# Starting the last stage of a three-stage graph kernel beside the second convolution's last closings, with the early edge terms split over two generators

## The chip, the cores and the metric

The kernel runs on 1 core of one Trainium2 chip. The metric is the device time of one execution in microseconds (us), lower being better. TensorE is called PE in the profile, VectorE DVE, ScalarE ACT, GpSimd POOL, and SP is the queue engine that issues most DMAs.

## The reference, cut to what matters

There are N = 12,500 nodes with 64 features, E = 200,000 edges sorted by destination, and 64 features on every edge.

```python
h = relu(layernorm(x))
g = relu(sage(h, W1l, W1r, b1))          # first convolution
x = x + sage(g, W2l, W2r, b2)            # second convolution
h = relu(layernorm(x))
# last stage, one message for every edge
m = relu(concat(h[src], h[dst], edge_attr) @ W1 + b1) @ W2 + b2
x = x + segment_mean(m, src)

def sage(x, Wl, Wr, b):
    mean = segment_sum(x[src], dst) / max(count(dst), 1)
    return mean @ Wl.T + b + x @ Wr.T
```

## The kernel before, in words

**Tiles and cells.** Nodes are put into 49 blocks of 256. The edges are sorted on the chip into 49 x 49 = 2401 cells, one for each pair (destination block, source block), with 128 slots. Gathers and segment sums are matmuls with one-hot matrices: `turned` (line 741) is made on VectorE from a row of node numbers that is spread over all partitions (`srow`, `drow`, line 731), and `hot` (line 750) from a column of them.

**Three stages.** The two convolutions are one loop over parts of 16 cells (lines 947 to 967): for each group of 4 cells, line 896 gathers into `got`, ScalarE copies it to `rows` (line 900), and three groups later line 775 adds it into a PSUM sum `acc`. `acc` has two buffers. Each time a row of 49 cells is full, a closing `conv` (lines 812 to 843) runs for that block of 256 nodes: a copy of the sums, a mean, a transposition (834), a matmul with the weights (839), and then `after_conv1` or `after_conv2`. The latter loads x (855), adds it (858), does a layer norm and makes the two tables of the last stage, `ta` and `tb` (864 to 884). The last stage (line 1144 on) goes in groups of 8 cells: matmuls into `got` (1077, 1078), `y` = gathered values plus edge terms (1081, 1083), ReLU (1086), two subtractions on GpSimd (1089), and sums three groups later by line 775. It goes through the 40 early source blocks in its first 1960 cells, and through the 9 late ones in the other 441.

**What sets the order.** Nothing is scheduled by a compiler: each engine executes its instructions in the order in which the Python code issues them. Steps are written as generators. `Line.tick` moves every open group or closing on by one `yield`, so that the work of several groups is mixed on each engine. `ahead` (line 911) loads the `srow`/`drow` of the first two parts, makes the first part's `turned`, and later loads two parts ahead.

**Edge terms.** `edge_terms` (lines 355 to 426) computes edge_attr @ W1 beside the main work. It loads edges of 4 blocks (3 blocks for the late ones) at a time by four (three) DMAs (369), transposes 4 (3) tiles (399), copies them (405), multiplies them (414), copies the result to `terms_o` (422) and then scatters it into DRAM tables by indirect DMAs on GpSimd's queue (382), each with an index column `turn_i` copied on VectorE (381). A unit of 4 tiles takes six steps and eight scatters. The class `Beside` takes a step whenever the cells passed, times a weight, add up to its pace: 4.45 per step with weights 1.1 and 0.9 per cell in the two convolutions, and 6.2 per step with weight 1 in the last stage. `rest()` takes all steps that are left at once. The early edge terms are 60 loads in one generator, which starts at cell 152 of the first convolution and goes on in the second. Its index table `pos` lies in the same pool, `terms`, on the right side of SBUF. Under this pacing it takes its last step at cell 2300 of the second convolution. The late generator takes its last step at cell 1904 of the last stage. When a generator ends, the scatters that are left are issued in one go (line 425).

**Between the stages.** After the second convolution's loop, line 968 takes all closings to their end, lines 969 and 970 reload what is left of `tb`, and only then do the pools `layers` (left side) and `terms` close and the pools of the last stage open. A pool that is opened where others were closed makes its first users wait for the last users of the old ones.

Of the kernel before, what the change touches and what calls it, by code (L numbers as in the profile page):

```python
# [9 lines left out]
FT = mybir.dt.float32  # L10
BF = mybir.dt.bfloat16
I32 = mybir.dt.int32
# [3 lines left out]
P = 128  # L16
# [98 lines left out]
def fast_path(  # L115
# [20 lines left out]
    N, D = x.shape  # L136
# [4 lines left out]
    NB = -(-N // BLK)  # L141
# [3 lines left out]
    CH = 7  # L145
# [16 lines left out]
    BJ = 5  # L162
    EARLY = J * BJ * HALVES
    LATE = NB - EARLY
    assert LATE > 0
# [188 lines left out]

    def edge_terms(work, psum, groups, ITEMS, U):


        loads = []
        for blocks in groups:
            step = ITEMS // len(blocks)  # L360
            loads += [(blocks, t0, min(step, TG - t0)) for t0 in range(0, TG, step)]

        def load(blocks, t0, m):
# [25 lines left out]
        before = iter(())  # L389
        ahead = load(*loads[0])  # L390
        for at, (blocks, t0, m) in enumerate(loads):
            e = ahead
# [32 lines left out]
        for _ in before:  # L425
            pass

# [70 lines left out]
    terms_work = terms_in.enter_context(tc.tile_pool(name="terms", bufs=2, side="right"))  # L498
    pos = terms_work.tile([P, EARLY, T], I32, name="pos", bufs=1)

    def pos_of(B):
        return pos[:, B] if B < EARLY else pos_late[:, B - EARLY]

# [219 lines left out]

    groups = [[*range(q, q + J)] for q in range(0, EARLY, J)]
    beside = Beside(edge_terms(terms_work, psum_x, groups, 12, 4), 4.45)


# [79 lines left out]
    work = layers.enter_context(tc.tile_pool(name="layers", bufs=2))  # L807
    next_rows = rows_with_one(work)
    line = Line()
    second = [None]  # L810

    def conv(layer, table, w, b, finish, B, acc):

        yield
        v = work.tile([P, 2, W3], FT, name="sums")
        nc.scalar.copy(v, acc[:, :, :W3])
        yield
        m = work.tile([P, 2, 2, D], FT, name="both")
        t = table[:, B]
# [13 lines left out]
        for h in range(2):  # L833
            nc.tensor.transpose(acc[:, h, :P], m[:, h].rearrange("p a d -> p (a d)"), ident)
        ct = work.tile([P, 2, P], FT, name="both_t")
        nc.scalar.copy(ct, acc[:, :, :P])
        yield
        for h in range(2):
            nc.tensor.matmul(acc[:, h, P:P + D], ct[:, h], w, start=True, stop=True)  # L839
        o = work.tile([P, 2, D], FT, name="conv")  # L840
        nc.vector.tensor_add(o, acc[:, :, P:P + D], rows(b, 2))
# [8 lines left out]
    def after_conv2(B, o):  # L850
# [31 lines left out]
        yield  # L882
        if not last:
            nc.sync.dma_start(of_block(b_mem, B), b)
            stored.add(B)
# [24 lines left out]

    def ahead(todo, load, turn):


        loaded = [load(p) for p in todo[:2]]
        made = {0: turn(todo[0], loaded[0])}
        for _ in made[0][1]:
# [11 lines left out]

    gathered, stored, present = [0], set(), set()

    def again():
        new = [B for B in range(gathered[0]) if B in stored and B not in present]
        if new and (len(new) >= CH or not line.all):
            B0 = new[0]
            B1 = next(B for B in range(B0, NB + 1) if B not in new or B == B0 + CH)
            nc.sync.dma_start(tb[:, B0:B1],
                              b_mem[B0 * BLK:B1 * BLK].rearrange("(b p h) d -> p b h d", p=P, h=2))
            present.update(range(B0, B1))
            return True

# [6 lines left out]
    for (layer, c0, c1, part), t, coming in ahead(  # L947
            todo, lambda p: sources(*p[:3]),
            lambda p, r: turned(work, "turned", r, p[2] - p[1])):
        for a, z in part:  # L950
# [6 lines left out]
            if layer or a >= 150:  # L957
                beside.passed((z - a) * (1.1, 0.9)[layer])
            if layer:
                gathered[0] = max(z - (CELLS - NB), 0)  # L960
                again()
        if layer == 0 and c1 == CELLS:
            for _ in chain(sorter, clearing):
                pass
            nc.vector.tensor_copy(which, bad)
            sorting.close()
            second[0] = layers.enter_context(tc.tile_pool(name="second", bufs=2))
    line.finish()
    while again():
        pass  # L970
    assert present == set(range(NB))
    beside.rest()
    layers.close()
    terms_in.close()

# [5 lines left out]
    late_in = ExitStack()  # L981
    late_work = late_in.enter_context(tc.tile_pool(name="late", bufs=2, side="right"))
    beside = Beside(edge_terms(late_work, psum_x, [[*range(B, min(B + LJ, NB))] for B in range(EARLY, NB, LJ)], 12, 3), 6.2)

    def keep(K, acc):

        v = late_work.tile([P, 2, W3], FT, name="sums")
        nc.scalar.copy(v, acc[:, :, :W3])
# [73 lines left out]
    def messages(last, e, p, ts, td, c0, a, z):  # L1062
# [3 lines left out]
        for c in range(n):  # L1066
            K, f = divmod(a + c, F)
            B = order[last][f]
            at = slice((a - c0 + c) * S, (a - c0 + c + 1) * S)
            for i, (lt, rt) in enumerate(((ts[:, 0, at], ta[:, K, 0]), (ts[:, 1, at], ta[:, K, 1]),  # L1070
# [35 lines left out]

    line = Line()
    summed = []

    under_way = [None]  # L1110
# [33 lines left out]
    for (last, c0, c1, part), (e, ts, td), coming in ahead(  # L1144
            [(last, *p) for last in range(2) for p in parts(G3, NB * len(order[last]))],
            lambda p: tuple(wait_rows(work, n, r[p[0]], p[1], p[2])
                            for n, r in (("srow", srow_k), ("drow", drow_k))), turned_both):
        if last and c0 == 2 * PART:
# [4 lines left out]
        for a, z in part:  # L1153
            around(lambda: line.tick_behind(messages(
                last, e, gather.tile([P, G3, 2 * D], FT, name="got"), ts, td, c0, a, z)))
            for _ in range(2):
                next(coming, None)
            if not last:
                beside.passed(z - a)
# [268 lines left out]
```

## Time and profile before

| | us |
|---|---|
| median of 3 runs | 3727.71 (3725.05 to 3731.02) |
| the profiled execution's own time | 3723.96 |
| its span in the trace | 3722.1 |
| first convolution, first to last gather | 93 to 1338 |
| second convolution, first to last gather | 1340 to 2305 |
| last stage, first matmul to the end | 2328 to 3722 |

| engine | busy us | share of the span |
|---|---|---|
| PE matmul | 3505.5 | 94% |
| PE weight load | 3423.2 | 92% |
| DVE | 3322.8 | 89% |
| POOL | 2732.6 | 73% |
| ACT | 2568.7 | 69% |

Shares are averages over three stages, so what a change in one place is worth has to be read from that place: from a table of busy time in chosen stretches, and from the list of instructions in order of time with the idle time before each of them and what ended it. In that list, "[4.11 <-DMA edges]" means that the engine had been idle for 4.11 us and that the landing of `edges` ended it. "PEclk" in the table of stretches is the share of TensorE's full clock that was granted.

### The profile page before, as it was taken

Reading aid. Unit: us, or ns where it says so; the run is one execution under the profiler, and the core shown is the slowest. Engines: PE = TensorE matmul, PEld = TensorE weight load, DVE = VectorE, ACT = ScalarE, POOL = GpSimd, SP = SyncE. Lnnn points to the kernel's source line nnn. Section 1 sums busy time; section 2 is a strip of 40 time slices with the busy share of each in tenths; the row PEclk is TensorE's granted clock in tenths of the full one; section 3 lists DMA queues with packets and bytes.
Section 4 is the critical chain, followed back from the end, with each engine's and each line's share of the span. In section 5 each row is a group of like instructions: output and inputs, shape, how many; then the busy total and the mean of one; then the engine's idle time right before and its main releaser. Section 6 shows DMA issues by size and latency. Waiting matters only on the chain.

```text
span 3722.1 us, 130679 instructions
## 1 busy us (share of the span) xinstructions
PE 3505.5 (94%) x51318; PEld 3423.2 (92%) x51318; DVE 3322.8 (89%) x7346; ACT 2568.7 (69%) x5875; POOL 2732.6 (73%) x2306
## 2 busy tenths in 40 slices
PE   1799999999999999999999998999999999998987
PEld 0799999999999999999999998899999999998887
DVE  7899999999999978888888887899999999998998
ACT  3466666666666667777777776688888888876665
POOL 4057787777778777777777774688888888996454
PEclk9999999999999999999999999999999999999999
DMA  6654555555454344444444444666666666666664
GB/s 209 247 169 148 159 153 157 156 157 156 137 166 151 116 129 141 136 136 144 136 131 140 139 132 131 227 215 203 217 214 212 203 216 210 208 196 193 196 213 138
DMA packets 413697, 635.90 MB, mean 171 GB/s; under 512 B 94131, under 2 KB 296247, under 8 KB 413070
## 3 DMA queue, kind: packets, MB, share of 16 engines
q1 hardware_dynamic: 353106, 572.87, 48.7%
q0 software_dynamic: 53312, 51.36, 4.6%
q8 instruction: 402, 6.59, 0.7%
q10 hardware_dynamic: 6652, 3.24, 0.4%
q14 instruction: 225, 1.84, 0.2%
HBM read 474.72 MB, written 155.83 MB: 169 GB/s over the span
## 4 chain that ended last, share of the span: by engine, by line
PE 75%; DVE 15%; DMA 4%; issue 3%; ACT 2%; POOL 1%; SPq 1%; DVEq 0%; POOLq 0%; ACTq 0%
PE acc L775 26%; PE got L896 17%; PE got L1077 11%; PE got L1078 6%; PE pE L414 4%; DVE hot L750 3%; DVE turned L741 2%; PE pE L399 2%; DVE hot_r L635 2%; PE pX L645 2%; DVE turned_d L741 1%; DMA terms_in<-terms 1%; PE acc L839 1%; PE got L1074 1%; PE pX L617 1%
## 5 line engine op out<-in xcount | busy, mean ns | idle before, releaser
L382 POOL DMA_INDIRECT terms<-terms_o,turn_i x1666 | 1937.7, 1163 | 663.3 <-issue 220.5
L900 ACT CAST rows<-got 128x384 bf16<-128x384 f32 x2402 | 1038.5, 487 | 592.3 <-PE got L896 577.7
L775 PEld LDWEIGHTS <-hot 128*128 128x128 bf16 x12006 | 1029.5, 98 | 19.0 <-issue 7.9
L775 PE MATMUL acc<-rows,hot 128*128 128x193 bf16 x9604 | 1006.0, 247 | 0.7 <-DVE hot L750 0.7
L1089 POOL TENSOR_TENSOR hidden<-hidden 128x512 f32<-128x512 f32 (+1 forms) x602 | 756.3, 1257 | 259.6 <-ACT hidden L1086 179.3
L896 PEld LDWEIGHTS <-turned 128*128 128x128 bf16 x9604 | 814.7, 98 | 67.4 <-issue 27.5
L750 DVE TENSOR_TENSOR hot<-dcol,local 128x1024 bf16<-128x1024 bf16 x1202 | 814.3, 682 | 4.1 <-PE acc L775 3.7
L741 DVE TENSOR_SCALAR turned<-srow,nid 128x2048 bf16<-128x2048 bf16 (+1 forms) x906 | 780.4, 875 | 21.1 <-issue 10.7
L1077 PE MATMUL got<-ta,turned 128*128 128x128 bf16 x3920 | 599.8, 220 | 7.3 <-DVE turned L741 7.3
L1077 PE MATMUL got<-tb,turned_d 128*128 128x128 bf16 x3920 | 600.7, 221 | 1.7 <-DVE turned_d L741 1.1
L1078 PE MATMUL got<-tb,turned_d 128*128 128x64 bf16 x3920 | 546.9, 193 | 0.0
L1078 PE MATMUL got<-ta,turned 128*128 128x64 bf16 x3920 | 546.5, 193 | 0.0
L896 PE MATMUL got<-ta,turned 128*128 128x192 bf16 x4802 | 499.7, 247 | 37.4 <-issue 24.8
L1097 ACT ACTIVATE hot_a<-every,scol 128x256 bf16<-128x256 bf16 x1200 | 507.0, 493 | 0.0
L896 PE MATMUL got<-tb,turned 128*128 128x192 bf16 x4802 | 494.1, 246 | 0.8 <-DVE turned L741 0.5
L1086 ACT ACTIVATE hidden<-y 128x512 f32<-128x512 f32 (+1 forms) x301 | 190.4, 632 | 293.5 <-DVE y L1083 169.5
L1077 PEld LDWEIGHTS <-turned 128*128 128x128 bf16 x3920 | 362.8, 98 | 8.2 <-issue 7.8
L1077 PEld LDWEIGHTS <-turned_d 128*128 128x128 bf16 x3920 | 360.2, 98 | 2.9 <-DVE turned_d L741 2.4
L1078 PEld LDWEIGHTS <-turned 128*128 128x128 bf16 x3920 | 359.5, 98 | 1.2
L1078 PEld LDWEIGHTS <-turned_d 128*128 128x128 bf16 x3920 | 359.9, 98 | 0.0
L741 DVE TENSOR_SCALAR turned_d<-drow,nid 128x2048 bf16<-128x2048 bf16 (+2 forms) x302 | 324.9, 1117 | 0.0
L1099 ACT ACTIVATE hot_a<-hot_a 128x1024 bf16<-128x1024 bf16 x300 | 317.2, 1057 | 9.5
(227 smaller groups left out, 5302.4 us busy)
## 6 DMA issues: line engine op xcount, KB each, us to landing
srow<-srow_b SPq DMA_DIRECT2D x300, 512.0 KB
srow<-srow_k SPq DMA_DIRECT2D x149, 512.0 KB
drow<-drow_k SPq DMA_DIRECT2D x149, 512.0 KB
terms_in<-terms SPq DMA_DIRECT2D x294, 160.0 KB
edges<-in_edge_attr_dram SPq DMA_DIRECT2D x200, 192.0 KB
terms<-tb SPq DMA_DIRECT2D x200, 160.0 KB
terms<-tb SPq DMA_DIRECT2D x48, 640.0 KB
terms<-terms_o,turn_i POOLq DMA_INDIRECT x1666
```

What stands on the lines that cost most here:

```text
L382: nc.gpsimd.indirect_dma_start(out=terms[j][:], out_offset=bass.IndirectOffsetOnAxis(ap=at, axis=0), in_=o[:, c, h], in_offset=None, bound ...
L741: nc.vector.tensor_scalar(o[:, h, :n * S], r[:, :n * S], nid[:, h:h + 1], None, op0=OP.is_equal)
L750: nc.vector.tensor_tensor(o[:, :n], cols.rearrange("p (g c) -> p g c", c=2).unsqueeze(2).to_broadcast([P, n, 2 * P, 2]), local.rearrange(" ...
L775: nc.tensor.matmul(self.acc[B][:, h, :W3], lt, r[:, c, 0:W3], start=k + h == 0, stop=k == row - 1 and h == 1, skip_group_check=True)
L896: nc.tensor.matmul(p[:, (i - c) * D3:(i - c + 1) * D3], t[:, h, (a - c0 + i) * S:(a - c0 + i + 1) * S], table[:, (a + i) % NB, h], start=h ...
L900: nc.scalar.copy(g[:, c:c + m, :D3], p[:, :m * D3].rearrange("p (c d) -> p c d", c=m))
L1077: nc.tensor.matmul(p[:, c], lt, rt[:, 0:2 * D], start=i == 0, stop=False, skip_group_check=True)
L1078: nc.tensor.matmul(p[:, c, 0:D], lt, rt[:, 2 * D:], start=False, stop=i == 3, skip_group_check=True)
L1086: nc.scalar.activation(w[:, :n, 0:D], y[:, :n], AF.Relu)
L1089: nc.gpsimd.tensor_sub(w[:, :n, (i + 1) * D:(i + 2) * D], w[:, :n, j], upper(w)[:, :n, j])
L1097: nc.scalar.activation(q[:, c - k], every, AF.Abs, scale=-1.0, bias=scol[:, scol_at[last] + a + c:scol_at[last] + a + c + 1])
L1099: nc.scalar.activation(q[:, :n - k], q[:, :n - k], AF.Relu, bias=1.0, scale=-2.0)
```

## The change

The early edge terms are made by two generators, of 33 and of 27 loads. The first is taken to its end when the first convolution ends (`beside.rest()`), and its pool closes. A new pool `second` is opened in that place, which holds the tiles of the second convolution's closings, and beside it a new pool `terms` for the second generator. The index table is split: blocks 0 to 19 in the old place, blocks 20 to 39 in `pos_second` in the pool `layers`. A generator begins with two empty steps behind its first load, and the last scatters of a generator are steps of their own. The weights go from 1.1 and 0.9 to 1.13 and 0.875.

At the end of the second convolution, closings are ticked only until the last sum is complete. Pools `terms` and `layers` close then, and the last stage begins: the first `srow` and `drow` loads, seven ticks of the closings, the first `turned`, and then four ticks behind each of the first groups of 8 cells, until no closing is left. Only then does the late generator start.

```diff
-    def edge_terms(work, psum, groups, ITEMS, U):
+    def edge_terms(work, psum, groups, ITEMS, U, only=slice(None)):
...
+        loads = loads[only]
...
         ahead = load(*loads[0])
+        yield
+        yield
...
         for _ in before:
-            pass
+            yield
...
-    pos = terms_work.tile([P, EARLY, T], I32, name="pos", bufs=1)
+    pos = terms_work.tile([P, J * BJ, T], I32, name="pos", bufs=1)
...
-    beside = Beside(edge_terms(terms_work, psum_x, groups, 12, 4), 4.45)
+    beside = Beside(edge_terms(terms_work, psum_x, groups, 12, 4, slice(FIRST)), 4.45)
...
+    pos_second.append(work.tile([P, J * BJ, T], I32, name="pos_second", bufs=1))
...
     def conv(layer, table, w, b, finish, B, acc):
 
+        work_ = second[0] if layer else work
...
-    def ahead(todo, load, turn):
+    def ahead(todo, load, turn, between=lambda: None):
 
         loaded = [load(p) for p in todo[:2]]
+        between()
...
-                beside.passed((z - a) * (1.1, 0.9)[layer])
+                beside.passed((z - a) * (1.13, 0.875)[layer])
...
             sorting.close()
-            second[0] = layers.enter_context(tc.tile_pool(name="second", bufs=2))
-    line.finish()
-    while again():
-        pass
-    assert present == set(range(NB))
+            beside.rest()
+            terms_in.close()
+            second[0] = seconds.enter_context(tc.tile_pool(name="second", bufs=2, side="right"))
+            terms_in = ExitStack()
+            terms_work = terms_in.enter_context(tc.tile_pool(name="terms", bufs=2, side="right"))
+            beside = Beside(edge_terms(terms_work, psum_x, groups, 12, 4, slice(FIRST, None)), 4.45)
     beside.rest()
+    gathered[0] = NB
+    while sums.acc:
+        line.tick()
+        again()
+    terms_in.close()
     layers.close()
-    terms_in.close()
+    ending, line = line, Line()
...
-            lambda p: tuple(wait_rows(...)), turned_both):
+            lambda p: tuple(wait_rows(...)), turned_both,
+            lambda: [ending.tick() for _ in range(7)]):
...
-            if not last:
+            if late_pool[0] is None:
+                for _ in range(4):
+                    ending.tick()
+                while again():
+                    pass
+                if not ending.all:
+                    assert present == set(range(NB))
+                    seconds.close()
+                    late_pool[0] = late_in.enter_context(tc.tile_pool(name="late", bufs=2, side="right"))
+                    beside = late(late_pool[0])
+            elif not last:
                 beside.passed(z - a)
```

More of the change, by code (lines that the diff above doesn't have):

```diff
@@ L163, in fast_path @@
     EARLY = J * BJ * HALVES
+    FIRST = 33
     LATE = NB - EARLY
@@ L498, in fast_path @@
     terms_work = terms_in.enter_context(tc.tile_pool(name="terms", bufs=2, side="right"))
-    pos = terms_work.tile([P, EARLY, T], I32, name="pos", bufs=1)
+    pos = terms_work.tile([P, J * BJ, T], I32, name="pos", bufs=1)
+    pos_second = []
     def pos_of(B):
-        return pos[:, B] if B < EARLY else pos_late[:, B - EARLY]
+        if B < J * BJ:
+            return pos[:, B]
+        return pos_second[0][:, B - J * BJ] if B < EARLY else pos_late[:, B - EARLY]
     sorting = ExitStack()
@@ L808, in fast_path @@
     next_rows = rows_with_one(work)
+    pos_second.append(work.tile([P, J * BJ, T], I32, name="pos_second", bufs=1))
     line = Line()
+    seconds = ExitStack()
     second = [None]
     def conv(layer, table, w, b, finish, B, acc):
+        work_ = second[0] if layer else work
         yield
-        v = work.tile([P, 2, W3], FT, name="sums")
+        v = work_.tile([P, 2, W3], FT, name="sums")
         nc.scalar.copy(v, acc[:, :, :W3])
         yield
-        m = work.tile([P, 2, 2, D], FT, name="both")
+        m = work_.tile([P, 2, 2, D], FT, name="both")
         t = table[:, B]
@@ L834, in conv @@
             nc.tensor.transpose(acc[:, h, :P], m[:, h].rearrange("p a d -> p (a d)"), ident)
-        ct = work.tile([P, 2, P], FT, name="both_t")
+        ct = work_.tile([P, 2, P], FT, name="both_t")
         nc.scalar.copy(ct, acc[:, :, :P])
@@ L839, in conv @@
             nc.tensor.matmul(acc[:, h, P:P + D], ct[:, h], w, start=True, stop=True)
-        o = work.tile([P, 2, D], FT, name="conv")
+        o = work_.tile([P, 2, D], FT, name="conv")
         nc.vector.tensor_add(o, acc[:, :, P:P + D], rows(b, 2))
@@ L882, in after_conv2 @@
         yield
-        if not last:
+        if last:
+            ready.add(B)
+        else:
             nc.sync.dma_start(of_block(b_mem, B), b)
@@ L926, in ahead @@
                     pass
-    gathered, stored, present = [0], set(), set()
+    gathered, stored, present, ready = [0], set(), set(), set()
     def again():
         new = [B for B in range(gathered[0]) if B in stored and B not in present]
-        if new and (len(new) >= CH or not line.all):
+        if new and (len(new) >= CH or gathered[0] == NB):
             B0 = new[0]
@@ L938, in again @@
             present.update(range(B0, B1))
+            ready.update(range(B0, B1))
             return True
@@ L981, in fast_path @@
     late_in = ExitStack()
-    late_work = late_in.enter_context(tc.tile_pool(name="late", bufs=2, side="right"))
-    beside = Beside(edge_terms(late_work, psum_x, [[*range(B, min(B + LJ, NB))] for B in range(EARLY, NB, LJ)], 12, 3), 6.2)
+    late = lambda late_work: Beside(edge_terms(late_work, psum_x, [[*range(B, min(B + LJ, NB))] for B in range(EARLY, NB, LJ)], 12, 3), 6.2)
     def keep(K, acc):
-        v = late_work.tile([P, 2, W3], FT, name="sums")
+        v = late_pool[0].tile([P, 2, W3], FT, name="sums")
         nc.scalar.copy(v, acc[:, :, :W3])
@@ L1068, in messages @@
             B = order[last][f]
+            assert {K, B} <= ready
             at = slice((a - c0 + c) * S, (a - c0 + c + 1) * S)
@@ L1105, in messages @@
         sums.add(o, upper(w), a, z, lambda *a: summed.append(((keep, last_sums)[last], a)), F, q)
-    line = Line()
     summed = []
+    late_pool = [None]
     under_way = [None]
@@ L1146, in fast_path @@
             lambda p: tuple(wait_rows(work, n, r[p[0]], p[1], p[2])
-                            for n, r in (("srow", srow_k), ("drow", drow_k))), turned_both):
+                            for n, r in (("srow", srow_k), ("drow", drow_k))), turned_both,
+            lambda: [ending.tick() for _ in range(7)]):
         if last and c0 == 2 * PART:
@@ L1157, in fast_path @@
                 next(coming, None)
-            if not last:
+            if late_pool[0] is None:
[9 more added lines that the diff above has]
+            elif not last:
                 beside.passed(z - a)
```

## Prediction

> **What bounds the kernel now.** I read the table of busy time in stretches first, cut at the stage borders that the first and last start times of the gather lines give.
>
> ```profile
> core 0: us, PE busy (x) PEld busy (x) DVE busy (x) ACT busy (x) POOL busy (x), PEclk, DMA share, GB/s
> 93.00:1339.00 1246.00, 1184.05 (x13863) 1133.03 (x13864) 1148.45 (x2894) 783.83 (x1962) 884.41 (x720) 1.00 0.51 158
> 1339.00:2306.00 967.00, 966.25 (x10978) 954.66 (x10976) 809.84 (x2348) 697.35 (x1880) 714.09 (x641) 1.00 0.44 138
> 2306.00:2329.00 23.00, 6.25 (x34) 3.78 (x32) 9.60 (x35) 5.72 (x20) 0.00 (x0) 0.60 0.35 108
> 2341.00:2346.00 5.00, 5.00 (x78) 5.00 (x76) 0.52 (x1) 0.24 (x1) 0.00 (x0) 0.62 0.72 261
> ```
>
> PE is the bound: 966.25 of 967 us in the second convolution, 1184 of 1246 in the first. So moving work between engines buys nothing there; only time in which PE stands still can be won. The one large hole is at the border before the last stage: 23 us with 6.25 us of PE work. There I read the list in order of time, all engines.
>
> ```profile
> 2305.15 2.35 PE L775 MATMUL acc<-rows,hot 128*128 128x193 bf16 x26
> ...
> 2313.15 0.17 DVE L853 MEMSET x<- 32x128 f32 x1
> ...
> 2323.30 0.32 SPq L731 DMA_DIRECT2D srow<-srow_k  x1
> ...
> 2327.34 1.42 DVE L741 TENSOR_SCALAR turned<-srow,nid 128x2048 bf16<-128x2048 bf16 x2 [3.60 <-DMA srow<-srow_k]
> ...
> 2328.67 1.41 DVE L741 TENSOR_SCALAR turned_d<-drow,nid 128x2048 bf16<-128x2048 bf16 x2
> ...
> 2334.89 0.69 DVE L1081 TENSOR_TENSOR y<-got,terms_in 128x512 f32<-128x512 f32 x1 [2.23 <-PE got L1078]
> ...
> 2338.97 0.48 PE L399 MATMUL pE<-ident,edges 128*128 128x128 f32 x1 [4.11 <-DMA edges<-in_edge_attr_dram]
> ...
> 2345.48 0.69 DVE L1081 TENSOR_TENSOR y<-got,terms_in 128x512 f32<-128x512 f32 x1 [6.46 <-PE got L1078]
> ...
> 2349.53 0.68 DVE L1081 TENSOR_TENSOR y<-got,terms_in 128x512 f32<-128x512 f32 x1
> ```
>
> The last sum ends at 2307.5. Then the closings of blocks 47 and 48 run alone, a chain of short operations with two loads of x in it; the last stage's first load goes out at 2323.30, its one-hot matrices are complete at 2330.08 (2328.67 + 1.41). Its second group is held up by the late generator, whose first transposition waits 4.11 us for its edges: the first two `y` are 10.6 us apart, the next two 4.05.
>
> The first border (1339) has no hole today. The rows that matter there after the change:
>
> ```profile
> 189.24 7.06 SPq L369 DMA_DIRECT2D edges<-in_edge_attr_dram  x7
> ...
> 195.16 0.33 PE L399 MATMUL pE<-ident,edges 128*128 128x128 f32 x1 [0.35 <-DMA edges<-in_edge_attr_dram]
> ...
> 1334.02 1.42 POOL L382 DMA_INDIRECT terms<-terms_o,turn_i  x1 [0.30 <-DVE turn_i L381]
> ...
> 1345.95 0.60 PE L399 MATMUL pE<-ident,edges 128*128 128x128 f32 x4
> ```
>
> And where the late generator ends, the same list shows what a run of scatters costs on GpSimd's queue:
>
> ```profile
> 3386.02 1.05 POOL L382 DMA_INDIRECT terms<-terms_o,turn_i  x1 [0.30 <-issue]
> 3389.96 0.97 POOL L382 DMA_INDIRECT terms<-terms_o,turn_i  x1 [2.90 <-DMA terms<-terms_o,turn_i]
> ...
> 3393.18 1.45 PE L775 MATMUL acc<-hidden,hot 128*128 128x193 bf16 x8 [6.79 <-POOL hidden L1089]
> ```
>
> **The change, part by part.** No operation is added or removed; order and waits change. Sums are made against the profiled execution, 3723.96 us (span 3722.1), which lies 3.75 under the median of 3727.71; I carry the difference over to the median.
>
> *A, the last stage's start.* In the changed order, SP issues the first four `srow`/`drow` loads ahead of block 48's load of x. They wait for the last reader of the pool `layers`, the sum ending at 2307.5. The first took 4.0 us (2323.30 to 2327.34), so 2311.5. On VectorE the three memsets of `hidden` (0.13 each) and seven ticks of closings stand ahead of `turned`; the last of these is L853, ending at 2313.3. So `turned` starts near 2313.7, not by its load, and needs 2.74 as traced (2327.34 to 2330.08): 2316.4 for 2330.08, a gain of 13.6. Behind x on SP, the first edge-term loads go out at 2313.7 and have until 2321. Late edge work starts only with cell 32, so the second `y` follows by 4.05, not 10.6: 6.5 more. Against this, seven VectorE operations of block 48 (0.17 + 6 x 0.29 = 1.9) now stand between the first four groups, each set waiting some 0.35 on ScalarE as traced: 3.0 in all. And late edge steps that lay in the first 56 cells (9, against one real step after) must be done later, on a busy PE: 8 steps are 1.33 units of 1.34 (three transpositions 0.49, six matmul passes 0.85), 1.8. A = 13.6 + 6.5 - 3.0 - 1.8 = 15.3. Bounds: 11, if each of the closing's four rounds through PE costs 1 more; 19, if the closings' operations all fall into waits.
>
> *B, the first border.* The second generator's pool lies on memory of the first. Its first `edges` load, third on SP behind the border, waits in the changed program for the first generator's last scatters on every lane. These are now one per step; five are issued by pace and three by `rest()` behind the border. The wait did not exist before. Eight scatters at 1.37 (median 1.07 and 0.30 issue) from 1334.0 end at 1344.7. A scatter's packets were written about 1.0 after its instruction (the one ending at 3390.93 until 3392.0): 1345.7. The fourth block's edges were usable 5.9 us after the first issue (189.24 to 195.16), since SP takes about 1 us for each: 1351.6. The first unit needs all four. The two empty steps put its transpositions where the old ones stood, 1345.95, less one L414 (1.08) that is gone, plus three index copies: 1345.3. PE waits 6.3 us, with everything behind it in order; nothing gives this back, as PE has no slack in this stage. Queued behind on SP are eight edge loads and then the next `srow`, not needed until some 6 us later. After such a wait PE ran at half clock: 0.62 in 2341 to 2346, which is 0.38 x 5 = 1.9 us lost. B = -8.2. Bounds: -3, if the scatters are done by the border; -12, if GpSimd is three scatters behind.
>
> The Trainium skill, "TensorE: Matmul & The Clock Gate", Part 1, says that an idle window of about 3.4 us halves the clock, and about 3.4 us of work restores it. This speaks against the change, as it opens a new hole of that length; an estimate from that page would make the loss 1.7 where the row gives 1.9.
>
> "DMA: Bandwidth & Descriptors", section "Anatomy of one DMA", puts a fixed cost of about 2 us on such a DMA, mostly the receipt of the write. If that stands where I have 1.0, B would be an estimated 1 us worse.
>
> *C, the late generator's end.* "Singly" does not hold there: with the start at cell 32, 309 of 315 steps are taken by cell 1952, and `rest()` issues the last five scatters at once, behind one more; before, seven stood in a row. The wait of 6.8 for `hidden` moves from cell 1912 to the change of tables and loses one scatter (1.4); but the edge terms of the next cells are now loaded behind those scatters (landing 1.0, loads 2 to 3). I take 0, bounds -4 and +3.
>
> *D, pacing.* Before, 556 of the steps fell into the first convolution, after it all 33 loads: 1.3 units more. Of their 2.2 us of PE time (0.60 + 1.08 each), taken from a stage with no idle PE, some falls into the first convolution's 62 us of idle PE, mostly short waits: +0.7, bounds -3 and +2.2.
>
> Splitting `pos` and moving the closings' tiles change no operation, and no engine's order by themselves: 0.
>
> Sum: 15.3 - 8.2 + 0 + 0.7 = 7.8. Execution 3716.2; median 3727.7 - 7.8 = **3719.9**.
>
> **Rivals.** *B absent*: GpSimd is up with its work, SP's wait falls away before the border. For it: the last scatters are spread over 16 us. Against it: three are issued behind the border in any case. 15 us, 3712.
>
> *Gain eaten*: A comes at its lower bound, 11, and C at -4, with B as above: 0 to 1, about 3727. For it: the burst keeps its shape, and now loads wait for it.
>
> *Slower: GpSimd's backlog at the first border.* Its queue starts a scatter every 1.4 us at the end of the first convolution, and the faster pace (1.13 for 1.10) asks for eight in about 10.3 us where it needs 11. With k scatters behind at the border, SP's wait and PE's hole grow by 1.4 k. At k = 6 the change gives nothing, at 12 it is over 0.2% slower, about 3736. For it: rows on GpSimd with 0.30 "issue" one after another. Against it: at 1334.02 it waited for a fresh index copy, so it had caught up.
>
> That the last stage does not begin earlier would need the `srow` load to wait for block 48's closing; the changed order puts it ahead.
>
> **Numbers.** 0.2%, 7.5 us, is about what a measurement of this kernel can tell from no change. Forecast as summed (gain 3 to 12): 0.45, a good half of it beyond 7.5; B absent: 0.19; gain eaten: 0.20; slower: 0.16, nearly all beyond. So faster 0.48, same 0.38, slower 0.14. The range reaches from A at its upper bound with little of B, a gain of 18 (3709.7), to a loss of 5 (3732.7).
>
> **What would show it.** First matmul of the last stage (L1077) about 7 us behind the last sum's end (2307.5) rather than 20.8; the first two `y` 4 to 5 us apart; no transposition ahead of cell 32; a wait of 5 to 8 us at the first L399 behind the first border, released by `edges`, at half clock after it; a wait of some 6 us for `hidden` still there, now at the change of tables. I am wrong if the border wait is under 3 or over 12, or if the last stage's first matmul still follows block 48's closing.

## The result, and the profile after

The changed kernel is slower: 3762.37 us (median of four runs, 3756.85 to 3767.29) against 3727.75 for the kernel before, a ratio of 1.0092 (95% interval 1.0080 to 1.0103). That is 34.6 us in the wrong direction, 0.9%, and beyond the upper end of my range (3732.7). The profiled execution took 3762.92 us with a span of 3761.0, 38.9 more than the span of before. The first and last start times of the gather lines cut both spans into the same four parts:

| us | first convolution, until its last gather | border and second convolution | from its last gather to the last stage's first matmul | last stage |
|---|---|---|---|---|
| before | 1338.3 | 966.8 | 23.2 | 1393.8 |
| after | 1369.9 | 994.1 | 9.8 | 1387.2 |
| difference | +31.6 | +27.3 | -13.4 | -6.6 |

The last stage does begin earlier, by 13.4 us where I had counted 13.6. Two losses ahead of it are larger.

First the busy time in stretches, cut at the same borders as before (columns as there).

```profile
93.00:1370.00 1277.00, 1198.25 (x13877) 1142.42 (x13878) 1151.61 (x2904) 784.75 (x1963) 901.86 (x732) 0.98 0.50 154
1374.00:1400.00 26.00, 7.10 (x58) 6.46 (x58) 9.39 (x23) 3.99 (x9) 17.68 (x18) 0.64 0.15 47
1400.00:2364.00 964.00, 960.72 (x10885) 948.47 (x10886) 796.90 (x2306) 692.53 (x1867) 687.39 (x608) 1.00 0.43 137
2366.00:2374.00 8.00, 2.93 (x16) 1.41 (x14) 5.22 (x21) 3.01 (x11) 0.00 (x0) 0.83 0.68 232
```

In the first convolution PE stands still for 79 of 1277 us; before it was 62 of 1246. These 17 us are about half of the 31.6. Most of the rest is busy time, 1198.25 us for 1184.05 on nearly the same number of matmuls, at a granted clock of 0.98 for 1.00. Behind the border there is a hole that before did not have: 7.10 us of PE work in 26. GpSimd (the fifth busy time) is at work through most of that hole. The hole before the last stage is down to 8 us.

The hole at the border, from the list in order of time:

```profile
1371.91 0.15 DVE L383 COPY turn_i<-pos_second 128x1 int32<-128x1 int32 x1 [2.83 <-DMA terms<-terms_o,turn_i]
...
1372.79 1.27 POOL L384 DMA_INDIRECT terms<-terms_o,turn_i  x1 [0.30 <-DVE turn_i L383]
1374.37 0.98 POOL L384 DMA_INDIRECT terms<-terms_o,turn_i  x1 [0.30 <-DVE turn_i L383]
...
1394.98 0.97 POOL L384 DMA_INDIRECT terms<-terms_o,turn_i  x1 [0.30 <-issue]
1396.26 0.97 POOL L384 DMA_INDIRECT terms<-terms_o,turn_i  x1 [0.30 <-issue]
1398.50 8.56 SPq L371 DMA_DIRECT2D edges<-in_edge_attr_dram  x8
1401.53 0.45 PE L403 MATMUL pE<-ident,edges 128*128 128x128 f32 x1 [17.31 <-DMA edges<-in_edge_attr_dram]
```

The mechanism is the one I described: SP's first `edges` load waits for the first generator's last scatter, and PE's first transposition waits for that load. Its length is not. The last gather of the first convolution starts at 1369.9; 20 scatters start behind it, nearly all of them with the usual 0.30 of idle time between them, and the last ends at 1397.2. I had counted eight from 4 us ahead of the border on, and had put the end of the last one 6 us behind it. The queue holds VectorE up as well (the first row), and the second convolution's first gather starts 4.1 us behind the last one of the first convolution; before, it was 1.3.

How many scatters GpSimd has in front of it can be counted: each has an index copy on VectorE ahead of it, so the copies started less the scatters started are the queue. Here are the rows of the two lines up to the last gather of the first convolution, first of before (until 1339), then of after (until 1370); the number behind the "x" of a row is the count.

```profile
L381 DVE COPY turn_i<-pos x732: 133/146/303, 208.0 to 1336.8; 128x1 int32<-128x1 int32 x183
L382 POOL DMA_INDIRECT terms<-terms_o,turn_i x720: 966/1084/2798, 209.0 to 1338.3; - x180
```

```profile
L383 DVE COPY turn_i<-pos x680: 133/145/369, 210.6 to 1270.9; 128x1 int32<-128x1 int32 x170
L383 DVE COPY turn_i<-pos_second x66: 134/146/155, 1273.2 to 1368.1; 128x1 int32<-128x1 int32 x66
L384 POOL DMA_INDIRECT terms<-terms_o,turn_i x732: 965/1086/2492, 211.6 to 1368.9; - x183
```

After has 746 - 732 = 14 in the queue at the border, and there are 16 buffers for index copies. But before, too, had 732 - 720 = 12. Its queue was 2, 3, 5, 9, 4, 8 deep at 400, 600, ..., 1200 and 1300; after's 7, 12, 11, 13, 12, 13. In 900 us from 400 to 1300 GpSimd did 574 scatters before and 571 after: asked for more, it did no more.

What a full queue does to the others shows in the waits of 400 to 930, of after:

```profile
POOL terms L384 <- DVE turn_i L383: 23.6, 64, 1.5
DVE turn_i L383 <- DMA terms<-terms_o,turn_i: 17.0, 15, 2.3
ACT terms_o L426 <- DMA terms<-terms_o,turn_i: 13.1, 11, 3.8
...
PEld pE L403 <- ACT terms_o L426: 5.2, 8, 1.9
```

VectorE waits for a free index buffer and ScalarE for a free `terms_o`, both held by scatters that GpSimd has not reached, and PE then waits for ScalarE. The same list of before has neither VectorE's nor ScalarE's wait.

Last, the start of the last stage: all engines until 2374.24, then VectorE's `y` alone.

```profile
2367.98 0.33 SPq L738 DMA_DIRECT2D srow<-srow_k  x1
...
2372.01 0.17 DVE L863 MEMSET x<- 32x128 f32 x1
2372.91 1.42 DVE L748 TENSOR_SCALAR turned<-srow,nid 128x2048 bf16<-128x2048 bf16 x2 [0.74 <-DMA srow<-srow_k]
...
2374.24 1.41 DVE L748 TENSOR_SCALAR turned_d<-drow,nid 128x2048 bf16<-128x2048 bf16 x2
```

```profile
2380.57 0.69 DVE L1101 TENSOR_TENSOR y<-got,terms_in 128x512 f32<-128x512 f32 x1 [0.55 <-PE got L1098]
...
2386.01 0.68 DVE L1101 TENSOR_TENSOR y<-got,terms_in 128x512 f32<-128x512 f32 x1
...
2391.82 0.68 DVE L1101 TENSOR_TENSOR y<-got,terms_in 128x512 f32<-128x512 f32 x1
...
2397.11 0.68 DVE L1101 TENSOR_TENSOR y<-got,terms_in 128x512 f32<-128x512 f32 x1
...
2401.14 0.68 DVE L1101 TENSOR_TENSOR y<-got,terms_in 128x512 f32<-128x512 f32 x1
```

The last sum's matmuls end at 2366.6 (2364.05 and 2.58). The first `srow` load goes out 1.4 us behind that, ahead of block 48's load of x. `turned` comes 0.74 behind the memset L863, and its row names the landing of `srow`: the load took 4.9 us (2367.98 to 2372.91), where I had 4.0 and took it to be through before the memset. The first two `y` are 5.4 apart instead of 10.6.

### The profile page after: what moved, and what is told of

It reads as the page before. It is cut to its first block, busy times and chain, and to the rows that moved or that the text cites. A ratio compares the mean times of both kernels' runs of the same rounds, so it can differ in the third digit from the quotient of the medians.

```text
span 3761.0 us, 130693 instructions
## 1 busy us (share of the span) xinstructions
PE 3517.4 (94%) x51318; PEld 3430.5 (91%) x51318; DVE 3307.1 (88%) x7346; ACT 2569.2 (68%) x5875; POOL 2738.7 (73%) x2306
## 4 chain that ended last, share of the span: by engine, by line
PE 54%; DVE 4%; DMA 3%; issue 1%; SPq 1%; ACT 0%; POOL 0%; DVEq 0%; ACTq 0%; POOLq 0%
PE acc L782 20%; PE got L1097 11%; PE got L908 10%; PE got L1098 6%; PE pE L418 3%; DVE turned_d L748 1%; PE pE L403 1%; PE got L1094 1%; DMA drow<-drow_k 1%; DMA terms_in<-terms 1%; DVE turned L748 1%; PE pX L879 1%; PE acc L849 1%; DVE y L1101 0%; DMA srow<-srow_k 0%
## 5 line engine op out<-in xcount | busy, mean ns | idle before, releaser
L748 DVE TENSOR_SCALAR turned<-srow,nid 128x2048 bf16<-128x2048 bf16 (+1 forms) x906 | 771.1, 865 | 15.3 <-issue 10.7
L1097 PE MATMUL got<-tb,turned_d 128*128 128x128 bf16 x3920 | 599.7, 220 | 2.9 <-DVE turned_d L748 2.9
L1097 PE MATMUL got<-ta,turned 128*128 128x128 bf16 x3920 | 598.8, 220 | 2.9 <-DMA drow<-drow_k 2.6
L908 PE MATMUL got<-ta,turned 128*128 128x192 bf16 x4802 | 503.8, 248 | 38.9 <-issue 24.7
L1097 PEld LDWEIGHTS <-turned 128*128 128x128 bf16 x3920 | 362.2, 98 | 3.3 <-issue 2.7
L1097 PEld LDWEIGHTS <-turned_d 128*128 128x128 bf16 x3920 | 359.5, 98 | 3.8 <-DVE turned_d L748 3.8
```

Source lines behind the costliest of these rows:

```text
L748: nc.vector.tensor_scalar(o[:, h, :n * S], r[:, :n * S], nid[:, h:h + 1], None, op0=OP.is_equal)
L908: nc.tensor.matmul(p[:, (i - c) * D3:(i - c + 1) * D3], t[:, h, (a - c0 + i) * S:(a - c0 + i + 1) * S], table[:, (a + i) % NB, h], start=h ...
L1097: nc.tensor.matmul(p[:, c], lt, rt[:, 0:2 * D], start=i == 0, stop=False, skip_group_check=True)
```

## The experiments

Theory T1: GpSimd's queue of scatters bounds the first convolution. The faster pace asks for more than it does, its queue stays full, and the full queue is what the border then waits for. Rivals: T2, the closing and reopening of the pool costs its 20 to 27 us whatever the queue; T3, the other order of instructions (two generators, two halves of `pos`) slows the first convolution; T4, the index copies have too few buffers; T5, the extra steps cost by their own work on PE, ScalarE and VectorE. The four parts of all profiled executions together, with medians and ratios to the kernel before, which ran beside them (its medians there 3725.56 to 3726.30):

| us | first conv. | border, second conv. | gap | last stage | median | ratio (95%) |
|---|---|---|---|---|---|---|
| pace_only | 1375.2 | 964.3 | 23.0 | 1392.0 | 3759.71 | 1.0093 (1.0076-1.0110) |
| old_pace_32 | 1346.1 | 993.9 | 10.3 | 1385.4 | 3737.30 | 1.0025 (1.0014-1.0035) |
| later_second | 1376.2 | 982.0 | 11.0 | 1388.2 | 3754.88 | 1.0068 (1.0051-1.0085) |
| more_index | 1357.7 | 993.5 | 10.6 | 1387.6 | 3758.96 | 1.0090 (1.0073-1.0107) |
| half_scatters | 1337.3 | 972.7 | 10.2 | 1388.1 | 3708.41 | 0.9953 (0.9937-0.9970) |
| before_slow | 1333.5 | 986.7 | 23.8 | 1391.8 | 3732.78 | 1.0012 (1.0003-1.0022) |
| less_first | 1332.0 | 980.6 | 19.8 | 1383.5 | 3719.59 | 0.9984 (0.9975-0.9994) |
| less_30 | 1328.7 | 991.3 | 30.2 | 1383.0 | 3742.39 | 1.0047 (1.0030-1.0064) |
| before_early | 1346.3 | 964.3 | 24.6 | 1388.9 | 3728.12 | 1.0003 (0.9994-1.0012) |
| combo_31 | 1331.4 | 973.7 | 21.1 | 1386.5 | 3715.07 | 0.9973 (0.9963-0.9983) |
| combo_32_early | 1336.9 | 972.5 | 9.5 | 1391.4 | 3711.23 | 0.9958 (0.9944-0.9971) |
| combo_32_early_more | 1351.1 | 968.8 | 15.8 | 1387.1 | 3725.86 | 0.9996 (0.9987-1.0005) |

One correction to the counts of steps in the expectations: I worked them out with 2450 cells for a convolution, and there are 2401. The steps by which a generator is said to be through before a border are therefore too many; by the right count less_first is four steps short at the first border, and combo_31, combo_32_early and combo_32_early_more are through 6, 1 and 5 steps before it.

**The pace alone, in the kernel before (pace_only).**

```diff
-                beside.passed((z - a) * (1.1, 0.9)[layer])
+                beside.passed((z - a) * (1.13, 0.875)[layer])
```

> The kernel before with one edit: the factors of the early generator's pace, 1.13 and 0.875 for 1.1 and 0.9. One generator, one pool, no early start of the last stage. Theory T1 (GpSimd's queue of scatters is full; the faster pace asks for more scatters than it takes, and VectorE, ScalarE and PE then wait for free buffers behind it): the last gather of the first convolution moves from 1338 to about 1368 (+25 to +33), `turn_i` L381 and `terms_o` L422 wait for scatters (some 20 to 40 us in sum between 400 and 1370), and the kernel takes 3750 to 3760. Theory T2 (the loss comes from closing and reopening the pool at the border): within 3 us of the kernel before. Theory T3 (the split of the generator and of `pos`, by its other order of instructions, slows the first convolution): within 3 us of the kernel before.

The first convolution ends at 1375.2, 36.9 later, `turn_i` and `terms_o` wait 34.7 and 29.1 us for scatters between 400 and 1330, and the time is 3759.71. With one generator and one pool, the pace costs about what the changed kernel loses there. Some 5 of the 36.9 are lost by 400 already (PE 275.00 busy in 93 to 400 for 279.78), where only 4 scatters are queued; these are not shown to be the queue's. T3 falls for the first convolution. The border costs nothing here (964.3): the queue of 14 stands there too, but no load waits for it.

**The old pace in the changed kernel (old_pace_32).**

```diff
-    FIRST = 33
+    FIRST = 32
...
-                beside.passed((z - a) * (1.13, 0.875)[layer])
+                beside.passed((z - a) * (1.1, 0.9)[layer])
```

> The changed kernel with the factors of the kernel before (1.1 and 0.9) and 32 and 28 loads in the two generators, so that all but one of the first generator's steps are taken by pace. Everything else of the change is kept. T1: the first convolution's last gather within 6 us of 1338, a wait of 3 to 10 for `edges` at the border, the early start of the last stage worth 18 to 22: 3710 to 3722, faster than the kernel before. T2: first convolution as before, 25 to 30 lost at the border: 3731 to 3738. T3: first convolution at 1365 or later: over 3745.

Most of T1's numbers are missed: the first convolution ends at 1346.1 (+7.8, I had allowed 6), and the border still has its hole. Around it:

```profile
1346.16 1.42 POOL L384 DMA_INDIRECT terms<-terms_o,turn_i  x1 [0.30 <-DVE turn_i L383]
...
1368.29 0.97 POOL L384 DMA_INDIRECT terms<-terms_o,turn_i  x1 [0.30 <-issue]
1370.54 8.57 SPq L371 DMA_DIRECT2D edges<-in_edge_attr_dram  x8
1373.05 0.45 PE L403 MATMUL pE<-ident,edges 128*128 128x128 f32 x1 [15.89 <-DMA edges<-in_edge_attr_dram]
```

Sixteen more scatters follow the one at 1346.16, for which only three index copies are still to come. So that scatter had not waited for its copy, although its row names one as releaser after 0.30 of idle time: 0.30 is what stands ahead of nearly every scatter of the two convolutions, with "issue" too. By the border's loss (27.1) and the time (3737.30), T2 would fit; the next experiments decide.

**Six empty steps before the second generator's first load (later_second).**

```diff
         before = iter(())
+        if only.start:
+            for _ in range(6):
+                yield
         ahead = load(*loads[0])
```

> The changed kernel with one edit: the second generator takes six empty steps before it issues its first load (some 30 us of its pace), so that neither SP nor PE has anything queued behind the first generator's last scatters at the border. Theory T1 for the border (PE's wait there is only for `edges`, which wait on SP for the pool's last scatters): the waits of 17 and more for `edges` L403 vanish, the first convolution stays at 1370, the border costs 3 to 6 instead of 27, and the kernel takes 3738 to 3745. Rival (what GpSimd owes has to be paid in any case, because the next scatters find full buffers): 3755 to 3763, the waits now on `turn_i` and `terms_o`.

The wait at the border does not vanish, as T1 had it, but falls from 17.3 to 5.7 us, by 11.6, and border and second convolution from 994.1 to 982.0. I had called six steps 30 us; at 0.875 a step stands for 5.09 cells of 0.40 us, so six are 12, just what was hidden. What hides there is a wait of fixed end, the last scatter; the cells behind the border have other work for PE. That is one reason why the time, 3754.88 (3745.00 to 3759.40), lies between both expectations; the other is a first convolution 6.3 longer than that of the changed kernel in the profiled execution.

**More buffers for index copies (more_index).**

```diff
-                    at = work.tile([P, 1], I32, name="turn_i", bufs=16)
+                    at = work.tile([P, 1], I32, name="turn_i", bufs=28)
```

> The changed kernel with one edit: 28 buffers for the index copies `turn_i` instead of 16 (three units and a half of scatters). T1: GpSimd's rate is the limit, so the wait of VectorE for `turn_i` goes (17 us in 400 to 930, to under 3), and that of ScalarE for `terms_o` grows instead; the first convolution's end moves by less than 10, the kernel takes 3752 to 3764. Rival (T4: the cost is VectorE's order being held up by a short ring of index copies, with everything behind it in its queue, not GpSimd's rate): first convolution's last gather at 1350 or earlier, 3740 or less.

As T1: VectorE's wait for `turn_i` is gone from the list of 400 to 930, that of ScalarE for `terms_o` grows from 13.1 to 17.6, and the time, 3758.96 (3751.48 to 3761.49), overlaps that of the changed kernel. The profiled execution is the fastest of the four. In it the first convolution ended 12.2 earlier, where T1 had allowed less than 10, and PE's wait at the border is longer (23.7 for 17.3), though border and second convolution together are not (993.5 for 994.1). A gain of a few us is therefore not excluded, but T4, which asked for 3740 or less, falls.

**Every second scatter left out (half_scatters).** This one decides. The order of all other instructions is that of the changed kernel, and so are its pools; only every second scatter of the first generator is left out, and with it the write that it makes.

```diff
-                    nc.gpsimd.indirect_dma_start(
+                    if only.stop is None or h == 0:
+                        nc.gpsimd.indirect_dma_start(
```

> The changed kernel, with every second scatter of the first generator left out (those with h = 1; their index copies and all work of PE, ScalarE and VectorE stay). Half of the edge terms of the first convolution's blocks are missing. T1 (GpSimd's rate alone holds the first convolution up, and its 14 queued scatters make the border's wait): the first convolution's last gather at 1330 or earlier instead of 1370, no waits for `turn_i` and `terms_o`, 6 or less lost at the border instead of 23, and 3695 to 3715 in all. Rival (T5: the extra steps of the faster pace cost by their work on PE, ScalarE and VectorE, whatever GpSimd does): the first convolution ends at 1360 or later, and the kernel takes 3740 or more.

Stretches of half_scatters (columns as above), and its list at the border:

```profile
93.00:1339.00 1246.00, 1187.86 (x13885) 1137.28 (x13885) 1148.01 (x2916) 783.18 (x1965) 491.79 (x376) 0.99 0.49 149
1339.00:1365.00 26.00, 21.43 (x207) 20.14 (x208) 14.72 (x30) 12.79 (x31) 2.13 (x2) 0.87 0.47 141
```

```profile
1338.92 1.98 POOL L385 DMA_INDIRECT terms<-terms_o,turn_i  x1 [0.31 <-DVE turn_i L383]
1343.52 8.56 SPq L371 DMA_DIRECT2D edges<-in_edge_attr_dram  x8
1346.54 0.30 PE L404 MATMUL pE<-ident,edges 128*128 128x128 f32 x1 [2.12 <-DMA edges<-in_edge_attr_dram]
```

The first convolution ends at 1337.3 instead of 1369.9, with the same steps; the border's wait is 2.12 instead of 17.31, with the same change of pools, and PE loses 4.6 us in the 26 behind it for 18.9. No wait of VectorE or ScalarE for a scatter is left in the first convolution. T2, T3 and T5 fall: both losses come from the number of scatters in GpSimd's queue. Whether GpSimd's own part of a scatter or the DMA behind it sets the rate is not separated, since both were left out together. The kernel takes 3708.41, so without most of that queue the early start of the last stage is worth some 18 net. My bound of 1330 was too low. With GpSimd out of the way PE is busy for 1187.86 of 1246 us and the end is that of the kernel before. This fits a kernel before that stood where both limits meet.

**Fewer steps in the first convolution (before_slow, less_first, less_30).** The kernel before with 1.06 and 0.94:

```diff
-                beside.passed((z - a) * (1.1, 0.9)[layer])
+                beside.passed((z - a) * (1.06, 0.94)[layer])
```

> The kernel before with the pace turned the other way: 1.06 and 0.94 for 1.1 and 0.9, so 21 steps fewer of the 568 before the border. T1 (in the kernel before, too, GpSimd has 5 to 13 scatters queued in the first convolution, and its queue is what the pace has to fit): queue at the border under 6, the first convolution's last gather at 1315 to 1328, the second 8 longer, in all 3713 to 3722. Rival (steps only move their PE work from one stage to the other): within 3 of the kernel before.

The changed kernel with six empty steps as above, 31 loads and the same factors, or 30 and (1.03, 0.97):

```diff
-    FIRST = 33
+    FIRST = 31
...
-                beside.passed((z - a) * (1.13, 0.875)[layer])
+                beside.passed((z - a) * (1.06, 0.94)[layer])
```

> The changed kernel with 31 and 29 loads in the two generators, the factors 1.06 and 0.94, and six empty steps before the second generator's first load. The first generator is then through some 10 steps (20 us) before the border. T1: its last scatters end near the border and no PE wait over 4 stands there; first convolution to 1320 to 1332, second 970 to 980, the gap before the last stage 10, the last stage 1387: 3697 to 3712, faster than both kernels. Rival (T2, the border costs some 20 whatever the queue): 3720 or more.

> As the run before it, one step further: 30 and 30 loads, the factors 1.03 and 0.97. T1: GpSimd's queue in the first convolution is short now (under 6 on the way), so that moving more steps away gains no more there (first convolution 1310 to 1325) and costs their PE work in the second (8 more): within 5 of the run with 31. Rival (the first convolution gains in proportion to the steps taken out of it, 1.5 us for each scatter): 10 or more faster than the run with 31.

less_first is the first version faster than the kernel before (3719.59), with a queue of 7 and a longest PE wait of 3.1 us at the border, though above T1's 3697 to 3712: its gap is 19.8, as scatters were left over at its end. The other two are slower, and T1's expectations for them were wrong: I had priced steps moved to the second convolution by their PE work and had not asked what GpSimd can take there. They missed in the first convolution too: before_slow ended it at 1333.5 (1315 to 1328 expected) with 9 to 11 scatters still queued, less_30 at 1328.7 (1310 to 1325 expected). Taking steps out of it gains little below the old pace. The waits of before_slow between 1400 and 2290:

```profile
DVE turn_i L381 <- DMA terms<-terms_o,turn_i: 66.5, 59, 2.5
POOL terms L382 <- DVE turn_i L381: 47.3, 117, 2.8
POOL terms L382 <- DMA terms<-terms_o,turn_i: 17.6, 51, 1.3
ACT terms_o L422 <- DMA terms<-terms_o,turn_i: 14.6, 13, 2.4
```

The queue is 12 to 14 deep there from 1600 on. From 1600 to 2200 GpSimd did 409 scatters, in less_30 414, one for every 1.45 to 1.47 us; the kernel before asked for 403, one for every 1.49, with a queue of 1 to 3. So the second convolution has the same limit, a little higher, and the old factors lie just under it. less_30 pays a second time at its end:

```profile
2342.02 0.97 POOL L384 DMA_INDIRECT terms<-terms_o,turn_i  x1 [0.30 <-issue]
2344.27 0.33 SPq L741 DMA_DIRECT2D srow<-srow_k  x1
```

The last stage's first `srow` load waits for the last scatter of the second generator, since that stage's pools lie on the generator's memory: the gap is 30.2 there.

**More time for GpSimd (before_early and three versions).** The early generator begun sooner; the rest as in the runs before:

```diff
-            if layer or a >= 150:
-                beside.passed((z - a) * (1.1, 0.9)[layer])
+            if layer or a >= 112:
+                beside.passed((z - a) * (1.082, 0.9)[layer])
```

> The kernel before, its generator begun at cell 112 of the first convolution instead of 150, with the factor 1.082 instead of 1.1, so that as many steps as before (568) fall ahead of the border. T1 (GpSimd's queue is what the pace has to fit, 13 scatters deep at the border before): the queue is 4 to 9 deep at the border, the first convolution ends 2 to 8 earlier, and the kernel takes 3718 to 3724. Rival (the queue costs nothing in the kernel before, since PE finds other work there): within 2 of the kernel before.

The changed kernel, with empty steps, `FIRST`, the first cell and the factors set so: combo_31 4, 31, 150, (1.08, 0.925); combo_32_early 4, 32, 100, (1.08, 0.91); combo_32_early_more 10, 32, 104, (1.09, 0.91).

> The changed kernel with 31 and 29 loads, the factors 1.08 and 0.925, and four empty steps before the second generator's first load: the first generator is through 20 steps (some 40 us) before the border, so its queue is empty there. T1: PE waits under 4 for `edges` at the border; the first convolution ends at 1328 to 1338, the second takes 972 to 980 (its 36 additional steps are 14 of PE work), the gap before the last stage 10 to 14 with few scatters left at its end, the last stage 1385: 3704 to 3716. Rival (T2, a wait of 15 or more at the border in any case): 3722 or more.

> The changed kernel with 32 and 28 loads, the factors 1.08 and 0.91, the first generator begun at cell 100 instead of 150, and four empty steps before the second generator's first load. The first generator is through 13 steps (some 27 us) before the border. T1: the queue is near empty at the border and at the end, PE waits under 6 at the border, the gap is 10, and the early start's gain of some 20 is what is left: 3700 to 3713. Rival (earlier scatters only fill the queue earlier, and 14 of them stand at the border as before): 3725 to 3738.

> As the run before it, with the first generator begun at cell 104, the factor 1.09 (through 17 steps before the border) and ten empty steps before the second generator's first load. T1: no wait for `edges` is left at the border, since the loads have 20 us; the second generator ends 5 steps before the second convolution does. 0 to 6 faster than the run before it where that one waits at the border; a longer gap before the last stage (over 12) if its scatters are late at the end.

before_early gained nothing (ratio 1.0003), as its rival had it, and its first convolution ended 8 later instead of 2 to 8 earlier: its queue is 9 to 10 at the border all the same, and at its new start PE waits 9.19 us for the first `edges`, since the old generator has no empty steps. combo_32_early is the best version of all, 3711.23, faster than the kernel before by 0.42% (0.29 to 0.56) and than the changed kernel by 51 us, all within T1's figures. Both its generators come out even (558 steps by pace for 557 needed, and 490 for 489). Around its border:

```profile
1345.17 1.06 POOL L384 DMA_INDIRECT terms<-terms_o,turn_i  x1 [0.30 <-DVE rcnt L840]
1347.62 3.73 SPq L371 DMA_DIRECT2D edges<-in_edge_attr_dram  x4
```

The last scatter ends at 1346.2, 9 us behind the last gather, and four empty steps cover most of the wait for the loads: PE waits under 1 us at each. combo_31, at 3715.07 still inside its range, loses 11 us of its gain in the gap: its second generator had 499 steps by pace for 507, so its last scatters are issued at once behind the others. combo_32_early_more (490 for 495) loses 6 there in the same way. It was expected to be 0 to 6 faster than combo_32_early and is 14.6 slower, since its first convolution is 14.2 longer, with the same work and a queue of at most 9 until 1330 (combo_32_early's reached 13 on the way). There VectorE waits 36.4 us in 37 pieces for the closings' matmuls (L854) until 1337, against 19.7 in 21: at another phase of the pace the steps may fall on other moments of the closings. Nothing tested what makes one phase better than another; that stays open, and with it differences of some 10 us between first convolutions that aren't held up by the queue.

## Why the prediction was wrong

By its own steps, in the span:

| step | predicted | measured | |
|---|---|---|---|
| A, start of the last stage | +15.3 (11 to 19) | +18.5 | size right |
| B, first border | -8.2 (-3 to -12) | -27.3 | mechanism right, size wrong |
| C, end of the late generator | 0 (-4 to +3) | +1.5 | size right, another wait |
| D, pacing | +0.7 (-3 to +2.2) | -31.6 | wrong |

Measured for D is the whole first convolution, for B the whole of border and second convolution.

**A** holds in size, in part by luck. `turned` starts 6.3 us behind the last sum's end, where I had 6.2 and before had 19.8, but by its load and not by the memsets and ticks ahead of it on VectorE; and the first L1097 follows 7.2 behind that end ("about 7"): 13.4 in the gap. Until the change of tables the stage then gains 11.9 (from the first L1097 to the first L1094: 1072.3 us for 1084.2). Of these 6.8 is the old wait for `hidden`, which belongs to C. 13.4 + 11.9 - 6.8 = 18.5. So behind the gap the stage gave 5.1, where my terms make 6.5 - 3.0 - 1.8 = 1.7; no run separates that. The closings between the first groups cost 4.5 instead of 3.0: the `y` are 5.4, 5.8 and 5.3 apart until the fourth, then 4.03.

**C** came out in size only. The wait of 6.8 is gone from its old place, and behind the change of tables 5.3 are lost. But what stands there is not PE's wait for `hidden`, as forecast; it is VectorE's for `terms_in`, which is loaded only while the late generator's last scatters run:

```profile
3446.03 0.97 POOL L384 DMA_INDIRECT terms<-terms_o,turn_i  x1 [0.30 <-issue]
...
3448.16 5.18 SPq L1150 DMA_DIRECT2D terms_in<-terms  x6
...
3448.62 1.05 POOL L384 DMA_INDIRECT terms<-terms_o,turn_i  x1 [0.30 <-issue]
...
3453.79 0.69 DVE L1101 TENSOR_TENSOR y<-got,terms_in 128x512 f32<-128x512 f32 x1 [4.96 <-DMA terms_in<-terms]
```

**D** is the step that failed. I took the additional steps of the first convolution (15 by pace, 1.3 units of real work) as PE work that fits into idle time, and put what they ask of GpSimd at nothing. GpSimd does one scatter in 1.57 us there (900/574), and it was near its limit already. By the rows above, 1129.3 us pass from its first scatter to the last gather before, with 720 scatters begun, and 1158.3 us after, with 732. The 12 more are 19 us of the 31.6; some 10 are a time per scatter that is 0.014 longer, which no run explains, and some 3 a later first scatter. That the scatters are the cause is shown by pace_only and half_scatters. My own row for GpSimd, 884.41 busy of 1246, looked like slack. It has almost none: the 0.30 ahead of every scatter isn't counted as busy, and for 720 scatters that is 216; with it 1100 us of the 1130 from the first scatter on are taken.

**B** had the right wait and mis-sized its first term: eight scatters from 1334.0 on with none ahead of them, where 20 started behind the last gather. What misled me was one sentence: "at 1334.02 it waited for a fresh index copy, so it had caught up". The row says [0.30 <-DVE turn_i L381], and 0.30 stands ahead of nearly every scatter; by the counts 12 were queued five microseconds later. The rival "GpSimd's backlog" had the right mechanism and nearly the right price at the border: 14 scatters at 1.4 would be 19.6, and PE lost 18.9 in the 26 us, of which 4.6 are left with half the scatters. Its "about 3736" at 12 behind is near the 3737.30 of old_pace_32, which has that queue without the faster pace; D's loss it did not have. I gave it 0.16 on the strength of that misread row. The clock's share behind the hole was right:

```profile
1401.00:1405.00 4.00, 1.74 (x5) 0.83 (x6) 0.00 (x0) 0.00 (x0) 0.00 (x0) 0.50 0.58 171
1405.00:1409.00 4.00, 4.00 (x28) 3.77 (x27) 0.69 (x1) 1.44 (x3) 0.00 (x0) 0.54 0.68 206
1409.00:1413.00 4.00, 4.00 (x47) 3.99 (x46) 1.39 (x2) 2.96 (x7) 0.00 (x0) 1.00 0.72 219
```

Behind the hole PE is granted half its clock until about 1409, some 4 us after it is busy throughout; 4 x 0.46 = 1.8 are lost, for 1.9 in my sum. The Trainium skill, "TensorE: Matmul & The Clock Gate", Part 1, says that about 3.4 us of sustained work bring the full clock back; the 4 us here are near that.

From the end of a pool's last scatter (start and duration of its row) to the next load that waits for it, SP needed 1.27 to 1.29 us (1397.23 to 1398.50, and likewise in old_pace_32, later_second, more_index and at less_30's end; 1.39 in combo_32_early, and 2.62 in half_scatters, which I can't explain). I had 1.0. The Trainium skill, "Perfetto Trace Analysis", section "DMA Instruction — SWDGE (GPSIMD)", says that the profile's end of such a DMA is the end of the writing of its descriptors and not of its data. The 1.27 lie behind that end; no run here shows what they are made of.

## What to carry over

A work generator that is paced by one engine's cells has to be priced on every engine it uses. Where one of them is near its limit, its service time for the work that is added is the first estimate of the cost; the other way round, taking work away gained little here. An in-order queue that is rarely idle can't be judged by its busy share or by the releaser named in its rows: count what was handed to it and what it has begun. A pool that is closed and reopened in mid-stream turns such a queue, which had cost nothing at that place, into a wait of its full depth, so let the old work run out before the border.

## What the runs showed of the hardware

The same scatter has different prices, counted from start to start: 1.28 us where the other engines stand still (1388.22, 1389.50, 1390.78, 1392.06 in the hole of after, rows of 0.97 with 0.30 ahead), 1.45 to 1.47 in a second convolution with a full queue, and 1.57 in the first convolution. In before, the rows are longer in the first convolution: 710.72 us for 574 scatters from 400 to 1300, a mean of 1.24, and 450.16 us for 403 from 1600 to 2200, a mean of 1.12. Some scatters wait for an earlier one's landing (12.0 us in 31 pieces between 400 and 930 of after). What makes the rows longer was not tried.
